# A four-layer scan network on one core: small VectorE operations moved or given PSUM operands, and the C product in three pieces

## The chip, the core and the metric

The kernel runs on one core of a Trainium2 chip. A core has engines that run side by side, each through its own queue in order: TensorE (PE, with weight loads shown apart as PEld), VectorE (DVE), ScalarE (ACT), GpSimd (POOL) and SyncE (SP), which here issues the DMAs. They meet in two memories on the chip: SBUF, and PSUM in eight banks of 512 float32 values per partition, which TensorE writes. The metric is the time of one execution in device microseconds; the time given for a kernel is the median of its runs.

## The reference

The input is 16 images of 192 channels by 32x32 pixels, all in float32. Four residual layers follow each other, each on a group norm of its input (32 groups of 6 channels):

```python
x = x + L0(_gn(x))   # mLSTM block over 1024 tokens, 12 heads of 32; a 3x3 convolution; batch norm; leaky ReLU
x = x + L1(_gn(x))   # Mamba block over 1024 tokens
x = x + L2(_gn(x))   # depthwise 3x3 convolution, batch norm over all images, clip to 0..6
x = x + L3(_gn(x))   # four-direction selective scan, and a local branch, mixed by a router
```

The scans of layers 1 and 3 are one recurrence, for 384 channels d and 16 states n:

```python
dA = jnp.exp(dt_t[..., None] * A)
h = dA * h + (dt_t * x_t)[..., None] * B_t[:, None, :]
y = jnp.einsum('bdn,bn->bd', h, C_t)
```

Layer 1 runs it once per image, layer 3 in four directions (rows and columns, forward and backward). The router of layer 3 is `softmax(x.mean((2, 3)) @ r_w.T + r_b)`, two weights per image, on the normalized image. Batch norm needs every image before any goes on, so layer 0 ends before layer 1 starts, and layer 2 before layer 3.

## The kernel before

**Layer 0** (lines 400 to 885) goes through the tokens in 128 chunks of 128. For each chunk TensorE forms the scores, VectorE multiplies them by the decays (line 765), TensorE sums them with the values into the PSUM tile `num`, and `layer0_norm` (line 833) normalizes each head: mean, square and variance on small 128x12 tiles. `layer0_state` carries a state of 128x396 from chunk to chunk. Fronts, group norms and the convolution are woven in between as side tasks.

**Layers 1 and 3** share `scan_run` (line 954). Its work is a list of steps; one step is one state n of one unit of 512 tokens, so layer 1 has 512 steps (2 units of 16 steps per image) and layer 3 has 2048 (8 units per image, 128 steps). In a step, the 384 channels are three tiles of 128 (t = 0, 1, 2). For each tile:

- ScalarE computes the decay `da` = exp(dt*A), 128x512 (line 991), and x*B in transposed form, `xbt` (line 971);
- TensorE turns `xbt` into the PSUM tile `xb`, three transposes and one product with a diagonal (lines 999, 1002; `xb` has 3 buffers), one step ahead of the scan;
- VectorE runs the recurrence over 512 tokens: `h` from `da` in SBUF and `xb` in PSUM (line 1015);
- GpSimd multiplies the whole `h`, 128x1536, in place by C, whose row for n was spread over the partitions by a DMA into `cb` (line 1022, called by `times_c` after the three scans); before it, it saves the last column as the carry for the next unit if there is one (line 1021);
- TensorE adds `h`, transposed, into the PSUM tile `y` (three banks), 4 transposes of 128x128 at a time (line 1033, `total`), two steps later. `h` has 4 buffers, each free again when `total` has read it.

After 16 steps `u.finish` takes `y` to SBUF (line 1141 on ScalarE in layer 1; line 1483 on ScalarE or 1485, an addition on VectorE, in layer 3). The diagonal for four states is made by GpSimd (line 981).

The order on each engine is what the program writes, but for small moves by the scheduler. The loop of `scan_run` (lines 1048 to 1060) writes scans, decays, turns and totals; between them `side.tick` runs the side tasks at the step numbers with which they were added: the next image's front, convolutions, projections and preparations, and the last image's tail. TensorE's scan work is chained in the written order (`in_order`). All side matmuls go through PSUM tiles named `mm`, of which there are two.

The lines of VectorE that the change touches are: `group_norm` (lines 350 to 379), the group norm's application in layer 0 (554), layer 1's front (1245, 1246, 1251) and tail (1368), layer 3's front (1558, 1562), its router (1697 to 1710) and mixing bias (1579, 1580), and in layer 0 the norm of a chunk (840 to 850) and the state (823 to 829). In layer 3 the front of the next image is a side task at steps 36.5 to 45 of the image before, and router and mixing bias come at step 45.

Of the kernel before, what the change touches and what calls it, by code (L numbers as in the profile page):

```python
# [19 lines left out]
HP = 96  # L20
# [259 lines left out]
class Program:  # L280
# [68 lines left out]
    def group_norm(self, pool, psum, x):  # L349
# [14 lines left out]
        d = pool.tile([HP, 2], F32, name="gnd")  # L364
        nc.vector.tensor_tensor(d, mv[:, :, 0], ps[:HP, :2], SUB)
        q = pool.tile([HP, 2], F32, name="gnq")
        nc.vector.tensor_tensor(q, d, d, MUL)
        nc.vector.tensor_tensor(q, q, mv[:, :, 1], ADD)
        mean = pool.tile([HP, 2], F32, name="gnmean")
        nc.vector.tensor_copy(mean, ps[:HP, :2])  # L370
# [3 lines left out]
        self.main.behind(nc.tensor.matmul(ps[:HP, :2], self.k("group", HP), q, start=True, stop=True))  # L374
# [4 lines left out]
        return mean, r, d  # L379
# [166 lines left out]
    def layer0_image(self, b, sp, bp, psum):  # L546
# [6 lines left out]
        for m in range(2):  # L553
            nc.vector.tensor_scalar(x[:, m], x[:, m], mean[:, m : m + 1], r[:, m : m + 1], SUB, MUL)
# [196 lines left out]
    def layer0_step(self, g, n, chunks, sp, bp, psum):  # L751
# [8 lines left out]
        if k:  # L760
# [27 lines left out]
            num = psum.tile([128, NH, DH + 1], F32, name="num", bufs=1)  # L788
# [20 lines left out]
        if k:  # L809
            self.layer0_norm(k, h, sp, bp)  # L810
            yield

    def layer0_state(self, k, vr, last, bp, psum):
# [3 lines left out]
        for i in range(3):  # L817
# [4 lines left out]
        new = k.state = bp.tile([128, 3, 132], F32, name="state")  # L822
        nc.vector.tensor_tensor(
            new, ps[:, :396].rearrange("p (i d) -> p i d", i=3),
            self.k0("bd")[:, None, :].to_broadcast([128, 3, 132]), MUL,
        )
        if last is not None:
            for i in range(3):
                nc.vector.scalar_tensor_tensor(
                    new[:, i], last.state[:, i], k.unit["dec"][:, i, k.c : k.c + 1], new[:, i], MUL, ADD  # L830
                )

    def layer0_norm(self, k, h, sp, bp):
# [6 lines left out]
        nc.vector.tensor_scalar(mean, mean, 1.0 / DH, None, MUL)  # L840
        hs = k.hs = bp.tile([128, NH, DH], F32, name="hs")
        nc.gpsimd.tensor_tensor(hs, x, mean[:, :, None].to_broadcast([128, NH, DH]), SUB)  # L842
        sq = bp.tile([128, NH, DH], F32, name="sq", bufs=1)
        nc.scalar.activation(sq, hs, AF.Square)
        d = sp.tile([128, NH], F32, name="den")
        nc.vector.tensor_tensor(d, h[:, :, DH], h[:, :, DH], MUL)
        nc.vector.tensor_scalar(d, d, 1.0, EPS, MAX, MUL)  # L847
        var = sp.tile([128, NH], F32, name="mhv")
        nc.vector.tensor_reduce(var, sq, AX.X, ADD)
        nc.vector.scalar_tensor_tensor(var, var, 1.0 / DH, d, MUL, ADD)  # L850
# [102 lines left out]
    def scan_run(self, units, side, bp, psum):  # L953
# [6 lines left out]
        xbt, xb, da, h = {}, {}, {}, {}  # L960
# [46 lines left out]
        def scan(i, t):  # L1007
            u, n = steps[i]
            first = u.carry_in is None
            if t == 0:  # L1010
                h[i] = bp.tile([128, 3, 512], F32, name="h", bufs=4)
# [5 lines left out]
        def times_c(i):  # L1017
# [710 lines left out]
```

## Time and profile before

| | |
|---|---|
| median of 3 runs | 17,061.52 us (17,039.57 to 17,072.65) |
| span of the profiled execution, first to last instruction | 17,013.7 us |
| busy: PE, PEld | 15,545.9 us (91%), 10,952.1 us (64%) |
| busy: VectorE, ScalarE, GpSimd | 13,117.0 (77%), 11,873.8 (70%), 11,405.1 us (67%) |
| mean granted TensorE clock | 0.960 |
| VectorE scans (line 1015) | 7,680, 9,092 us together |
| GpSimd C products (line 1022) | 2,560, 8,866 us, 3,467 ns each |

The profile is of one execution, whose own whole time is not on the page; its span is 47.8 us shorter than the median of the runs, which holds what lies before the first and after the last instruction as well. In a row of the groups, the name of the line and engine is followed by output and inputs, the shapes, the number of instructions, the busy time in all and the mean of one, and then the time that the engine stood idle just before them and what ended it. In a table of stretches, the busy time of each engine stands beside the stretch's length: an engine near 100% of it sets its time. A short operation with a long duration was held up while it was already counted as busy.

### The profile page before, as it was taken

To read this page: it belongs to the slowest core of one execution; us is meant where nothing else is said; L and a number is where in the kernel's file an instruction comes from. 1 tells how busy PE (TensorE), PEld (TensorE's weight loads), DVE (VectorE), ACT (ScalarE), POOL (GpSimd) and SP (SyncE) were. 2 spreads that over 40 slices of the span, in tenths; PEclk is the share of its full clock that TensorE was granted. 3 is DMA by queue.
4 is the path that set the end of the run, shared out by engine and by line. 5 is a ranking of instruction groups with operands and counts; after the bars stand their busy time and mean duration, and the time that the engine had idled before them with its cause. 6 is when DMAs were issued, how large, how long until landed. Compare 5 with 4: busy or idle time off the path is not lost. (4 is left out here: it accounts for less than half of the span.)

```text
span 17013.7 us, 263068 instructions
## 1 busy us (share of the span) xinstructions
PE 15545.9 (91%) x99452; PEld 10952.1 (64%) x99452; DVE 13117.0 (77%) x14795; ACT 11873.8 (70%) x19766; POOL 11405.1 (67%) x5491
## 2 busy tenths in 40 slices
PE   8999999989999999879999999999999999999998
PEld 4444444446666666557777777777777777777777
DVE  4555455447777877668888988888888888888888
ACT  3333333337677777558888888888888888888888
POOL 3434444436555555558888878888887888888888
PEclk8999999989999999989999999999999999999999
DMA  1111111123444444333323323332332333233232
GB/s 52 47 46 46 47 46 43 45 78 108 121 124 124 124 123 124 94 110 99 110 83 100 108 90 96 103 104 88 100 109 85 98 108 95 95 102 108 83 99 66
DMA packets 890140, 1544.64 MB, mean 91 GB/s; under 512 B 83472, under 2 KB 314653, under 8 KB 879530
## 3 DMA queue, kind: packets, MB, share of 16 engines
q1 hardware_dynamic: 888874, 1527.81, 29.5%
q8 instruction: 788, 12.91, 0.3%
q14 instruction: 478, 3.92, 0.1%
HBM read 1284.22 MB, written 243.27 MB: 90 GB/s over the span
## 5 line engine op out<-in xcount | busy, mean ns | idle before, releaser
L1022 POOL TENSOR_TENSOR h<-h,cb 128x1536 f32<-128x1536 f32 x2560 | 8866.4, 3467 | 1531.8 <-DVE h L1015 1020.4
L991 ACT ACTIVATE da<-dt,neg_a 128x512 f32<-128x512 f32 x7680 | 5265.6, 714 | 1549.4 <-DVE h L1015 1499.2
L1015 DVE TENSOR_TENSOR_SCAN h<-da,carry,xb 128x512 f32<-128x512 f32 x3840 | 4648.8, 1262 | 703.1 <-PE xb L1002 619.0
L1033 PE MATMUL y<-const,h 128*128 128x128 f32 x30720 | 4705.2, 276 | 115.6 <-DVE ysum L1485 54.0
L1015 DVE TENSOR_TENSOR_SCAN h<-da,xb 128x512 f32<-128x512 f32 x3840 | 4443.4, 1202 | 431.9 <-PE xb L1002 269.0
L999 PE MATMUL xb<-const,xbt 128*128 128x128 f32 x23040 | 4055.0, 281 | 293.6 <-DVE h L1015 155.7
L971 ACT ACTIVATE xbt<-ut,bt 128x384 f32<-128x384 f32 x7680 | 4168.0, 603 | 220.2 <-PE xb L999 219.5
L1033 PEld LDWEIGHTS y<-const,h 128*128 128x128 f32 x30720 | 3674.0, 143 | 315.3 <-issue 263.1
L999 PEld LDWEIGHTS xb<-const,xbt 128*128 128x128 f32 x23040 | 2749.4, 142 | 1743.1 <-issue 568.6
L1002 PE MATMUL xb<-diag,ut 128*128 128x128 f32 x15360 | 3006.1, 278 | 0.0
L1002 PEld LDWEIGHTS xb<-diag,ut 128*128 128x128 f32 x15360 | 2374.7, 195 | 55.9 <-issue 55.9
L842 POOL TENSOR_TENSOR hs<-h,mhm 128x384 f32<-128x384 f32 x128 | 108.6, 848 | 1567.2 <-DVE den L847 731.8
L981 POOL TENSOR_TENSOR diag<-const,bt 128x512 f32<-128x512 f32 x640 | 681.3, 1065 | 522.6 <-PE xb L1002 331.8
L1021 POOL COPY carry<-h 128x3 f32<-128x3 f32 x1280 | 244.3, 191 | 1167.3 <-DVE h L1015 999.6
L531 PE MATMUL conv<-ya,w_conv 128*64 128x512 f32 (+1 forms) x1152 | 502.2, 647 | 102.8 <-DMA ya<-yrows 57.8
L716 POOL TENSOR_TENSOR e<-e,const 128x1536 f32<-128x1536 f32 x128 | 443.4, 3464 | 223.8 <-DMA e<-row 207.7
L928 PE MATMUL mm<-dbl,w_dt 45*128 45x512 f32 x960 | 537.1, 643 | 49.9 <-DVE dt L932 26.8
L722 ACT ACTIVATE e<-e 128x1536 f32<-128x1536 f32 x128 | 189.8, 1482 | 420.9 <-POOL e L717 420.8
L791 PEld LDWEIGHTS num<-v,p 128*128 128x128 f32 x3072 | 385.7, 200 | 123.0 <-issue 51.2
L1182 PE MATMUL mm<-rep,t_dw 96*32 96x512 f32 x2304 | 432.4, 625 | 23.6 <-DMA rep<-xr 23.5
L1182 PE MATMUL mm<-rep,taps 128*32 128x512 f32 x3072 | 421.9, 609 | 26.1 <-DMA rep<-xr 15.9
L580 PE MATMUL mm<-xn,w_up 96*128 96x512 f32 x768 | 400.6, 667 | 35.9 <-DVE xn L398 28.3
(273 smaller groups left out, 17311.8 us busy)
## 6 DMA issues: line engine op xcount, KB each, us to landing
cb<-row SPq DMA_DIRECT2D x2560, 256.0 KB
rep<-xr SPq DMA_DIRECT2D x384, 331.0 KB
e<-row SPq DMA_DIRECT2D x128, 768.0 KB
rep<-xin SPq DMA_DIRECT2D x384, 256.0 KB
rep<-xr SPq DMA_DIRECT2D x384, 228.8 KB
xr<-xin SPq DMA_DIRECT2D x48, 612.5 KB
xr<-xpad SPq DMA_DIRECT2D x32, 867.0 KB
x<-x SPq DMA_DIRECT2D x32, 768.0 KB
```

Of the source, the lines that this page charges most:

```text
L531: nc.tensor.matmul(o, self.w_c2[:k, t, c0 : c0 + o.shape[0]], src[:k, r0 : r0 + 16, dx : dx + W], start=t == 0, stop=t == 14, skip_group_c ...
L716: nc.gpsimd.tensor_tensor(k.e, k.e, self.k0("mask")[:, None, :].to_broadcast([128, NH, 128]), ADD)
L928: nc.tensor.matmul(ps, w_dt[:, t * 128 : (t + 1) * 128], dbl, start=True, stop=True)
L971: nc.scalar.activation(t[:, c], u.ut[:, c], AF.Copy, scale=u.bt[:, c, n : n + 1])
L981: nc.gpsimd.tensor_tensor(d, ident[:, None, :].to_broadcast([128, 4, 128]), u.bt[:, 3, n : n + 4][:, :, None].to_broadcast([128, 4, 128]), ...
L991: nc.scalar.activation(da[i, t], u.dt[:, t], AF.Exp, scale=u.neg_a(t, n))
L999: in_order(nc.tensor.transpose(xb[i, t][:, c * 128 : (c + 1) * 128], xbt[i][:, c, t * 128 : (t + 1) * 128], ident))
L1002: in_order(nc.tensor.matmul(xb[i, t][:, 384:], u.ut[:, 3, t * 128 : (t + 1) * 128], u.diag[n // 4][:, n % 4], start=True, stop=True, skip_ ...
L1015: nc.vector.tensor_tensor_scan(hv, dv, xv, 0.0 if first else u.carry_in[:, n, t : t + 1], MUL, ADD)
L1022: nc.gpsimd.tensor_tensor(h[i], h[i], u.c.pop(n)[:, None, :].to_broadcast([128, 3, 512]), MUL)
L1033: in_order(nc.tensor.matmul(u.y[:, j], h[i][:, t, c * 128 : (c + 1) * 128], ident, is_transpose=True, start=n == 0 and j % 4 == 0, stop=n ...
L1182: self.nc.tensor.matmul(ps[32 * g : 32 * g + 32], blocks[:, g * side + r], seen, start=r == 0, stop=r == side - 1, skip_group_check=True,)
```

## The change

Five things change. The diff is cut to them.

1. **The C product**: three products of 128x512, each written after its own scan, from `h` into a new tile `hc`. `h` and `hc` have two buffers each, in place of four of `h`. `h` is released by GpSimd's last piece and the carry copy, `hc` by TensorE. The transposes into `y` come one step after the scan in place of two, four for the same t at a time, and `y` is laid out by t first.
2. **Group norm**: difference, square and sum of the small tiles go from VectorE to ScalarE's Square (two of 96x1) and to TensorE, which adds the variance by a second matmul. The mean is kept negated. Applying it goes from VectorE to ScalarE in layer 0 and to GpSimd in layers 1 and 3.
3. **Fronts of layers 1 and 3**: the leaky or clipped branch passes through a PSUM tile `mm`, so that VectorE has one input in SBUF and one in PSUM; layer 1's addition goes to GpSimd.
4. **Router and mixing bias of layer 3**: two-input operations become reductions over two elements, ScalarE steps, and two small GpSimd operations.
5. **Layer 0**: the chunk's mean and one square go to ScalarE; square and sum of squares live in spare columns of the PSUM bank of `num`; the state's decay is applied on the PSUM tile before the mask, not on the SBUF state after it.

```diff
@@ group_norm
-        nc.vector.tensor_tensor(d, mv[:, :, 0], ps[:HP, :2], SUB)
-        nc.vector.tensor_tensor(q, d, d, MUL)
-        nc.vector.tensor_tensor(q, q, mv[:, :, 1], ADD)
+        for m in range(2):
+            nc.scalar.activation(q[:, m : m + 1], ps[:HP, m : m + 1], AF.Square, bias=mv[:, m, 0:1], scale=-1.0)
-        nc.vector.tensor_copy(mean, ps[:HP, :2])
+        nc.vector.tensor_scalar(mean, ps[:HP, :2], -1.0, None, MUL)
...
-        self.main.behind(nc.tensor.matmul(ps[:HP, :2], self.k("group", HP), q, start=True, stop=True))
+        self.main.behind(nc.tensor.matmul(ps[:HP, :2], self.k("group", HP), mv[:, :, 1], start=True, stop=False))
+        self.main.behind(nc.tensor.matmul(ps[:HP, :2], self.k("group", HP), q, start=False, stop=True))
...
@@ layer0_image
-            nc.vector.tensor_scalar(x[:, m], x[:, m], mean[:, m : m + 1], r[:, m : m + 1], SUB, MUL)
+            nc.scalar.activation(shift, mean[:, m : m + 1], AF.Copy, scale=r[:, m : m + 1])
+            nc.scalar.activation(x[:, m], x[:, m], AF.Identity, bias=shift, scale=r[:, m : m + 1])
@@ layer0_state
-        nc.vector.tensor_tensor(
-            new, ps[:, :396].rearrange("p (i d) -> p i d", i=3),
-            self.k0("bd")[:, None, :].to_broadcast([128, 3, 132]), MUL,
-        )
+        add = ps[:, :396].rearrange("p (i d) -> p i d", i=3)
...
-                    new[:, i], last.state[:, i], k.unit["dec"][:, i, k.c : k.c + 1], new[:, i], MUL, ADD
+                    add[:, i], last.state[:, i], k.unit["dec"][:, i, k.c : k.c + 1], add[:, i], MUL, ADD
...
+        nc.vector.tensor_tensor(new, add, self.k0("bd")[:, None, :].to_broadcast([128, 3, 132]), MUL)
@@ layer0_norm
-        nc.vector.tensor_scalar(mean, mean, 1.0 / DH, None, MUL)
+        nc.scalar.activation(mean, mean, AF.Copy, scale=1.0 / DH)
...
+        nc.scalar.activation(n2, h[:, :, DH], AF.Square)
...
-        nc.vector.tensor_tensor(d, h[:, :, DH], h[:, :, DH], MUL)
-        nc.vector.tensor_scalar(d, d, 1.0, EPS, MAX, MUL)
+        nc.vector.tensor_scalar(d, n2, 1.0, EPS, MAX, MUL)
...
-        nc.vector.tensor_reduce(var, sq, AX.X, ADD)
-        nc.vector.scalar_tensor_tensor(var, var, 1.0 / DH, d, MUL, ADD)
+        nc.vector.tensor_reduce(ss, sq, AX.X, ADD)
+        nc.vector.scalar_tensor_tensor(var, ss, 1.0 / DH, d, MUL, ADD)
@@ scan_run
-                h[i] = bp.tile([128, 3, 512], F32, name="h", bufs=4)
+                h[i] = bp.tile([128, 3, 512], F32, name="h", bufs=2)
...
-        def times_c(i):
-            nc.gpsimd.tensor_tensor(h[i], h[i], u.c.pop(n)[:, None, :].to_broadcast([128, 3, 512]), MUL)
+        def times_c(i, t):
+                hc[i] = bp.tile([128, 3, 512], F32, name="hc", bufs=2)
+            nc.gpsimd.tensor_tensor(hc[i][:, t], h[i][:, t], u.c[n], MUL)
...
             for t in range(3):
                 scan(i, t)
+                times_c(i, t)
                 decay(i + 1, t)
                 turn(i + 1, t)
-                total(i - 2, t)
+                total(i - 1, t)
...
-            times_c(i)
@@ layer1_front
+                nc.scalar.activation(ps, v, AF.Copy, scale=0.01)
-                nc.vector.scalar_tensor_tensor(v, v, 0.01, v, MUL, MAX)
-                nc.vector.tensor_tensor(x[:, m, h], x[:, m, h], v, ADD)
+                nc.vector.tensor_tensor(v, v, ps, MAX)
+                nc.gpsimd.tensor_tensor(x[:, m, h], x[:, m, h], v, ADD)
...
-            nc.vector.tensor_scalar(xf[:, m], x[:, m], mean[:, m : m + 1], r[:, m : m + 1], SUB, MUL)
+            nc.gpsimd.tensor_scalar(xf[:, m], x[:, m], mean[:, m : m + 1], r[:, m : m + 1], ADD, MUL)
@@ layer3_front (layer1_tail's last operation alike)
+                nc.scalar.activation(ps, y2[:, h], AF.Relu, bias=self.bn2[:, m, 1:2], scale=self.bn2[:, m, 0:1])
+                nc.vector.scalar_tensor_tensor(x[:, m, h], ps, 6.0, x[:, m, h], MIN, ADD)
...
-            nc.vector.tensor_scalar(
+            nc.gpsimd.tensor_scalar(
                 xpad[:, m, 1 : 1 + W, 1 : 1 + W], x[:, m].rearrange("p (a b) -> p a b", b=W),
...
+        nc.gpsimd.tensor_tensor(xm, d, mean, ADD)
+        nc.gpsimd.tensor_tensor(xm, xm, r, MUL)
@@ layer3_local, router
-        nc.vector.scalar_tensor_tensor(wb, self.v96("3pw_b", 0, 2), wts[:, 1:2], wb, MUL, ADD)
+            nc.scalar.activation(wb[:, m : m + 1], self.v96("3b_out", m), AF.Copy, scale=wts[:, 0:1])
...
-        nc.vector.tensor_tensor(xm, d, r, MUL)
-            nc.vector.tensor_copy(wide, xm[:, m : m + 1].to_broadcast([HP, HP]))
+            nc.scalar.copy(wide, xm[:, m : m + 1].to_broadcast([HP, HP]))
...
-        nc.vector.tensor_tensor(top, e[:, 0:1], e[:, 1:2], MAX)
-        nc.vector.tensor_scalar(e, e, top, None, SUB)
-        nc.scalar.activation(e, e, AF.Exp)
-        nc.vector.tensor_tensor(top, e[:, 0:1], e[:, 1:2], ADD)
+        nc.vector.tensor_reduce(top, e, AX.X, MAX, negate=True)
+        nc.scalar.activation(e, e, AF.Exp, bias=top)
+        nc.vector.tensor_reduce(top, e, AX.X, ADD)
```

## The prediction

> **What bounds the kernel now.** I read the busy time by stage first (layer 0 ends at 3739 us, layer 1's scan run at 7160, layer 3's run goes from 7390 to 16948), then the same table for one image of layer 3, then VectorE and GpSimd in order of time, then the waits. Columns of the table: stretch, its length, busy us of PE, PEld, DVE, ACT, POOL, granted clock, DMA share, GB/s.
>
> ```profile
> 0.00:3739.00 3739.00, 3331.78 (x14599) 1718.78 (x14600) 1841.11 (x3649) 1146.42 (x1733) 1436.26 (x876) 0.91 0.19 49
> 3739.00:7160.00 3421.00, 3152.74 (x19115) 2106.66 (x19115) 2696.69 (x2916) 2458.09 (x4000) 2056.94 (x986) 0.98 0.39 118
> 7390.00:16948.00 9558.00, 8891.84 (x65173) 7064.64 (x65171) 8515.84 (x8122) 8214.00 (x13958) 7883.04 (x3611) 0.98 0.31 97
> ```
>
> Layers 0 and 1 are PE's (89% and 92%). In layer 3, four engines are between 82 and 93% busy, so the bound changes from stretch to stretch. One image of it (128 steps):
>
> ```profile
> 12205.00:12400.00 195.00, 173.01 (x1232) 139.46 (x1231) 170.14 (x167) 173.31 (x290) 159.68 (x77) 0.98 0.24 74
> 12400.00:12447.00 47.00, 34.69 (x232) 31.20 (x230) 46.83 (x49) 31.29 (x57) 32.44 (x19) 0.85 0.38 125
> 12447.00:12744.00 297.00, 294.09 (x2168) 220.54 (x2167) 256.62 (x242) 251.46 (x425) 243.53 (x114) 0.99 0.36 114
> 12744.00:12807.00 63.00, 58.21 (x473) 51.49 (x472) 61.61 (x56) 59.81 (x107) 57.81 (x19) 1.00 0.25 79
> ```
>
> The second row, 8 steps of 5.9 us, is VectorE alone: 46.83 of 47.00. It holds the next image's front, group norm and router. The third is PE's; the last, 16 steps of 3.9 us with little side work, is VectorE's with GpSimd 92% busy. VectorE in the second row, in order of time (start, us, instruction):
>
> ```profile
> 12402.15 3.48 DVE L1558 SCALAR_TENSOR_TENSOR x<-tmp,x 96x512 f32<-96x512 f32 x1
> ...
> 12418.70 1.85 DVE L367 TENSOR_TENSOR gnq<-gnd 96x2 f32<-96x2 f32 x1
> ...
> 12428.90 2.76 DVE L1697 TENSOR_TENSOR xm<-gnd,gnr 96x2 f32<-96x2 f32 x1
> ...
> 12435.46 2.47 DVE L1705 TENSOR_TENSOR rt<-re 96x1 f32<-96x1 f32 x1
> ...
> 12442.09 2.40 DVE L1580 SCALAR_TENSOR_TENSOR wb<-p,re,wb 96x2 f32<-96x2 f32 x1
> ```
>
> Two elements per partition in 2.76 us is a wait, not work: line 1697 alone spreads from 149 to 2775 ns (min/median/max, from its own view), up to the length of GpSimd's long product, which runs meanwhile:
>
> ```profile
> L1697 DVE TENSOR_TENSOR xm<-gnd,gnr x16: 149/2748/2775, 7289.0 to 16036.9; 96x2 f32<-96x2 f32 x16
> ```
>
> The product's price whole, and the nearest row for a piece of it (same engine, operation and 128x512 shape), then four products back to back:
>
> ```profile
> L1022 POOL TENSOR_TENSOR h<-h,cb 128x1536 f32<-128x1536 f32 x2560 | 8866.4, 3467 | 1531.8 <-DVE h L1015 1020.4 <-issue 308.0 <-DMA rep<-xin 39.7
> L1152 POOL TENSOR_TENSOR sz<-sz,o 128x512 f32<-128x512 f32 x96 | 122.3, 1274 | 38.8 <-DVE o L1151 38.5
> ```
>
> ```profile
> 12001.22 13.73 POOL L1022 TENSOR_TENSOR h<-h,cb 128x1536 f32<-128x1536 f32 x4
> ```
>
> **A. Layer 3's front and router.** VectorE loses per image, from its rows over 16 images: line 1558 (64 x 1555 ns, to be 740 like line 1688's PSUM form) 52 us; 1562 42; 1697 39; 1580 and 1579 39; 367 30; 1705 25 (a reduce of 0.17 stays); 1700 10; 1706, 1708 and 1710 10; 365 and 368 4: 252 us, 15.7 per image. The second row's VectorE falls to 31 us. GpSimd gets two 96x1024 operations (between 1.83, scaled from line 717's 2752 ns for 1536, and line 611's 2352; 2.1 taken), two tiny ones (0.19, line 1021) and the pieces' 8 x 0.26 (D): 32.4+4.6+2.1 = 39.1 us. So GpSimd bounds the stretch next, at 39.7 us if it fills 98.5%, as the busiest engine does in the rows beside it: -7.3 us on 15 images (the first front runs before the run, uncontended), -110 us. Ends: 0 (GpSimd comes out late and hands the time on) and -15.7 x 15 = -235.
>
> **B. Layer 1.** Lines 1246, 1251, 1368 and 367 cost VectorE 12.5 us per image there; but PE was 92% busy, and in a stretch with four 1246s in 5.43 us (5208 to 5228) PE was busy 17.5 of 20.0 and VectorE 18.7. I take that 2 us and a little of the tail: -2.3 x 15 = -35; ends 0 and -12.5 x 15 = -188.
>
> **C. Layer 0.** Line 850 (128 x 0.5 us over its median 0.17) and 554 (32 x 1.45 over its unblocked 0.80) give VectorE back 110 us, but it is 49% busy and PE 89%. Against that, mean and square take 256 ScalarE steps at 0.21 us (line 851), which lengthen each chunk's chain by 54 us in all. The state's decay on PSUM keeps an "mm" tile three operations (1.2 us) longer, with 24 matmuls of scores behind it as cover. Taken 0; ends -110 and +54.
>
> **D. The product in pieces.** A piece costs 1.272 (line 1152, in place: I take out of place as equal, no row shows it). Back to back, starts lie 0.05 closer ((13.73-3.47)/3 = 3.42). So 3 x 1.225 = 3.67 in place of 3.42: +0.26 us of GpSimd a step, 650 us in all. What hides it is GpSimd's idle time (18% in layer 3); what breaks the cover is burstiness: a quick step takes VectorE 3.5 us (nine scans in 10.65), while GpSimd needs 3.67 plus 0.26 for the diagonal's share plus, in the units that hand a carry on, 0.27: 3.9 to 4.2. It falls behind 0.4 to 0.7 a step. The h ring, cut from four tiles to two, allows about 2.1 us (three scans less one piece and the carry) before a step's first scan must wait, with VectorE's whole queue behind it. y one step behind is no loss: the first piece is done 1.27 after its scan and asked for a whole step later, where the whole product left some 1.3 us. Laid over the recorded scan ends of all 2,560 steps (a piece starts after its scan and the piece before; a step's first scan waits for the last piece of two steps back; each lack moves everything behind it), starts 1.227 apart lose 84 us, 1.16 apart 4, 1.30 apart 238. I take +84, by the row of the same shape; ends +238 and -73 (PE's 57.2+16.0 us of waits for the whole product, gone).
>
> [...]
>
> **E. New waits.** 128 front tiles (lines 1245, 1558) go through the two-deep "mm" ring between ScalarE and VectorE, and PE queues behind. The like wait, PE for line 932, cost 54 us over 480 tiles: 128 x 0.11 = +14; ends 0 and 128 x 0.74. The stores of x1, xf1 and xpad now wait for GpSimd in SP's queue with the cb loads behind; at its 60% load in layer 1 I cost that at nothing (48 x 2.6, the longest cb wait, if cover fails: 125). One more matmul per group norm: 64 x 2 passes x 0.224 = 29 if bare, +10 taken. The drain is a step and two pieces shorter: -3.
>
> **Sum:** -110-35+0+84+14+10-3 = -40. The profiled span is 17,013.7; the median of the runs, 17,061.5, lies 47.8 above it (start and end), which I leave. 17,061.5-40, rounded: 17,020.
>
> **Rivals.** *GpSimd becomes the bound* (slower): for it, its 92% in the last row above and the halved ring; against it, the 18% idle. Decides when starts of pieces lie over about 1.26 apart: at 1.30, D is +238, A shrinks to -60, B stays: 17,061+238-60-35+24 = 17,230. *The relief is paid in full* (faster): freed VectorE stops delaying scans in layers 0 and 1 too: A -150, B -100, C -50, D +40, the rest +21: -239, so 16,820. For it, the 550 us of VectorE time in A to C; against it, PE at 92%. *Nothing moves*: the engines change places and time hangs on PE (294.09 of 297.00 in the third row): 17,060.
>
> **How the numbers follow.** Forecast case 0.5 (16,900 to 17,070 by itself; of it 0.40 faster, 0.10 within 0.2%, which is about what a measurement tells from no change), GpSimd bound 0.32 (0.02 of it within 0.2%), full relief 0.10, nothing moves 0.08 (0.03 within, 0.05 slower by small costs). Faster 0.50, same 0.15, slower 0.35. The range leaves out the far halves of the outer cases: 16,840 to 17,230.
>
> **What would show it.** A: no VectorE operation of two elements over 0.4 us; the eight front steps at about 40 us, GpSimd the busiest. D: pieces at 1.27 us, GpSimd near 90% in layer 3, and a first scan of a step waiting for GpSimd, 50 to 150 us in all; pieces near 1.1 would make it faster, waits over 250 us slower. E: PE waits for line 1251's successor. C: layer 0 within 60 us of 3,739. Wrong most easily by the piece's price and by how long the front's new GpSimd work holds products up.

## The result and the profile after

| | before | after |
|---|---|---|
| median | 17,050.24 us (12 runs) | 17,031.19 us (12 runs, 17,009.24 to 17,052.04) |
| ratio | | 0.9988 (95% interval 0.9979 to 0.9996) |
| span of the profiled execution | 17,013.7 us | 17,028.0 us |
| layer 0, layer 1, between, layer 3, tail | 3,739, 3,416, 234, 9,554, 70 us | 3,741, 3,430, 236, 9,553, 69 us |

The change takes 19 us off, 0.12%; 40 were forecast. The stages of the two profiled executions hardly differ (layers 1 and 3 are taken from their first scan to the first scan of their last step), so the question is not where the 19 us are but what cancels what. A stage's time is that of one profiled execution: layer 0, whose code is the same in six of the kernels of this document, takes 3,740 to 3,755 us in them, so that 10 us between two stages say little by themselves. A first look is the busy time by stage of the changed kernel, with the same columns as before: stretch, length, busy us of PE, PEld, DVE, ACT, POOL, granted clock, DMA share, GB/s.

```profile
0.00:3741.00 3741.00, 3346.38 (x14638) 1726.58 (x14639) 1612.96 (x3291) 1250.86 (x2092) 1430.60 (x882) 0.91 0.19 49
3741.00:7175.00 3434.00, 3159.53 (x19185) 2088.58 (x19184) 2515.02 (x2720) 2499.98 (x4120) 2327.66 (x2130) 0.98 0.41 118
7406.00:16963.00 9557.00, 8903.37 (x65212) 7053.84 (x65211) 8306.00 (x7937) 8252.77 (x14100) 8411.10 (x7766) 0.98 0.33 97
```

VectorE lost 228 us of work in layer 0, 182 in layer 1 and 210 in layer 3; GpSimd gained 271 and 528 in the last two. The length of every stage stayed. One image of layer 3 in the same four stretches shows that something did move:

```profile
12203.00:12398.00 195.00, 174.22 (x1216) 142.06 (x1215) 169.31 (x166) 172.25 (x288) 170.13 (x157) 0.96 0.25 75
12398.00:12440.00 42.00, 32.61 (x239) 26.43 (x238) 32.26 (x38) 33.43 (x67) 37.89 (x41) 0.97 0.40 129
12440.00:12737.00 297.00, 293.85 (x2171) 221.35 (x2170) 256.61 (x241) 250.95 (x423) 256.35 (x238) 1.00 0.38 116
12737.00:12802.00 65.00, 58.54 (x478) 52.08 (x477) 62.55 (x57) 61.37 (x110) 61.96 (x52) 1.00 0.25 75
```

The front stretch went from 47 to 42 us, and VectorE in it from 46.83 to 32.26. But now no engine fills it: GpSimd, the busiest, has 37.89 of 42.00. The last stretch, quiet steps, is 2 us longer. The small operations of that front in order of time (start, us, instruction) are not held up any more:

```profile
12399.59 0.66 DVE L1563 SCALAR_TENSOR_TENSOR x<-mm,x 96x512 f32<-96x512 f32 x1
...
12427.17 0.15 DVE L1714 TENSOR_REDUCE rt<-re 96x1 f32<-96x2 f32 x1
```

None of VectorE's operations on one or two elements in the group norms and the router takes over 0.16 us in this kernel.

The groups of the changed kernel give the prices of the new operations: a piece of the product 1,279 ns, a branch on VectorE 667, a group norm applied on GpSimd 1,202. In the first line GpSimd's idle time before the pieces is nearly all waiting for TensorE to free `hc`.

```profile
L1022 POOL TENSOR_TENSOR hc<-h,cb 128x512 f32<-128x512 f32 x7680 | 9582.1, 1279 | 1609.6 <-PE y L1038 1460.7 <-DVE h L1016 105.5 <-issue 21.7
...
L1563 DVE SCALAR_TENSOR_TENSOR x<-mm,x 96x512 f32<-96x512 f32 x64 | 42.6, 667 | 37.5 <-ACT mm L1562 37.5
...
L1567 POOL TENSOR_SCALAR xpad<-x,gnmean,gnr 96x1024 f32<-96x1024 f32 x32 | 38.1, 1202 | 0.7 <-ACT gnr L376 0.7
```

The waits (in all, times, longest, us) show what is new. First TensorE's and VectorE's in the changed kernel, then the two of TensorE's that answer them in the kernel before:

```profile
PE mm L1186 <- DMA rep<-xr: 118.9, 41, 11.0
PE y L1038 <- DVE ysum L1491: 102.2, 45, 3.2
...
DVE h L1016 <- POOL hc L1022: 151.7, 146, 4.6
DVE h L1016 <- POOL carry L1027: 95.5, 94, 3.0
```

```profile
PE y L1033 <- DVE ysum L1485: 54.0, 32, 2.7
PE mm L1182 <- DMA rep<-xr: 39.4, 25, 10.0
```

`rep` are the shifted copies of the padded image that the depthwise convolutions of layers 2 and 3 read; they are loaded from `xr`, which is stored from `xpad`. TensorE waits for them three times as long as before, and twice as long for the addition of a finished unit's `y` to the sum (`ysum`).

Cut into 8 steps (first scan to first scan), the mean over images 0 to 14 of layer 3 shows gains at two places and losses at many, in us:

| steps | before | after | difference |
|---|---|---|---|
| 24 to 32 | 38.23 | 33.85 | -4.38 |
| 40 to 48 (front, router) | 46.72 | 42.28 | -4.44 |
| 0 to 8, 64 to 72, 96 to 104 | 120.38 | 123.47 | +3.09 |
| 32 to 40, 48 to 56 | 73.34 | 75.59 | +2.25 |
| 112 to 120 | 31.97 | 33.22 | +1.25 |
| last image, whole | 529.5 | 549.5 | +20.0 |

In layer 1 (images 1 to 14), steps 28 to 32 went from 29.58 to 34.03 us, which is +62 us and more than the stage lost. The experiments take these apart. Their phases are always those of this table.

### The profile page after: what moved, and what is told of

Same layout as the page of the kernel before. It is cut to its first block, busy times and chain, and to the rows that moved or that the text cites. A ratio compares the mean times of both kernels' runs of the same rounds, so it can differ in the third digit from the quotient of the medians.

```text
span 17028.0 us, 269290 instructions
## 1 busy us (share of the span) xinstructions
PE 15578.2 (91%) x99580; PEld 10929.7 (64%) x99580; DVE 12493.1 (73%) x14043; ACT 12059.5 (71%) x20391; POOL 12201.4 (72%) x10803
## 5 line engine op out<-in xcount | busy, mean ns | idle before, releaser
L1022 POOL TENSOR_TENSOR hc<-h,cb 128x512 f32<-128x512 f32 x7680 | 9582.1, 1279 | 1609.6 <-PE y L1038 1460.7
L1038 PE MATMUL y<-const,hc 128*128 128x128 f32 x30720 | 4715.8, 276 | 157.4 <-DVE ysum L1491 102.2
L1038 PEld LDWEIGHTS y<-const,hc 128*128 128x128 f32 x30720 | 3663.2, 143 | 365.8 <-POOL hc L1022 248.6
L393 PE MATMUL mm<-lnsq,const 96*96 96x512 f32 (+1 forms) x576 | 348.2, 689 | 87.0 <-ACT lnsq L392 64.0
```

The source lines that it names most:

```text
L1022: nc.gpsimd.tensor_tensor(hc[i][:, t], h[i][:, t], u.c[n], MUL)
L1038: in_order(nc.tensor.matmul(u.y[:, t, c], hc[i][:, t, c * 128 : (c + 1) * 128], ident, is_transpose=True, start=n == 0 and c == 0, stop=n ...
```

## Experiments: the moves and the pieces, each alone

**The moves alone**: the scan loop of before, everything else as after.

```diff
-            nc.gpsimd.tensor_tensor(hc[i][:, t], h[i][:, t], u.c[n], MUL)
+            nc.gpsimd.tensor_tensor(h[i], h[i], u.c.pop(n)[:, None, :].to_broadcast([128, 3, 512]), MUL)
...
-                total(i - 1, t)
+                total(i - 2, t)
...
+            times_c(i)
```

> The changed kernel with the scan loop of before (one product of 128x1536 in place, y two steps behind, four h buffers); all moves of VectorE's small operations kept. If relief and pieces simply add (my theory), this is 60 to 150 us faster than before: the eight front steps of layer 3 fall from 46.7 to about 40 us per image, and step 24 of an image of layer 3 stays at 11.0 us, since GpSimd's queue is as coarse as before. Rival, the relief is worth little by itself because TensorE takes the place of VectorE: within 30 us of before, front steps at 44 us or more.

**The pieces alone**: the reverse, the kernel before with the scan loop of after.

```diff
-            nc.gpsimd.tensor_tensor(h[i], h[i], u.c.pop(n)[:, None, :].to_broadcast([128, 3, 512]), MUL)
+            nc.gpsimd.tensor_tensor(hc[i][:, t], h[i][:, t], u.c[n], MUL)
...
-                total(i - 2, t)
+                total(i - 1, t)
```

> The kernel before with only the new scan loop (three out-of-place pieces, y one step behind, h and hc two buffers each); VectorE's small operations as before. If relief and pieces add: 40 to 130 us slower than before, step 24 of an image of layer 3 down from 11.0 to about 7.4 us (GpSimd's queue is finer), quiet steps about 1 us longer per 8. Rival, the shorter product already shortens the holds on VectorE: no two-element operation of VectorE over 1.4 us, front steps of layer 3 at 43 us or less, the whole within 30 us of before or faster; then the two halves overlap and their sum is more than the whole.

| | median, us | ratio (95%) | layer 1 | layer 3 | 40 to 48 | 24 to 32 |
|---|---|---|---|---|---|---|
| both (after) | 17,031.19 | 0.9988 (0.9979 to 0.9996) | 3,430 | 9,553 | 42.28 | 33.85 |
| moves alone | 16,942.38 | 0.9939 (0.9926 to 0.9951) | 3,443 | 9,467 | 39.87 | 37.49 |
| pieces alone | 16,976.12 | 0.9961 (0.9948 to 0.9973) | 3,381 | 9,539 | 39.71 | 34.80 |

A ratio is to runs of the kernel before that were taken beside the run; where ratio and medians differ, the ratio counts. Each alone is faster than both together. The front falls to the same 39.8 us by either, but not to the same limit. The front stretch of image 8 with the pieces alone, then with the moves alone:

```profile
12369.00:12409.00 40.00, 31.21 (x219) 27.64 (x219) 39.83 (x50) 27.57 (x50) 33.34 (x34) 0.87 0.43 137
12368.00:12408.00 40.00, 31.20 (x230) 25.03 (x229) 30.98 (x36) 33.20 (x67) 35.92 (x23) 0.97 0.41 131
```

With the pieces alone VectorE still fills the stretch, with less to hold it up. With the moves alone it has 30.98 of 40.00 us, no engine fills the stretch, and TensorE waits in it for the copies `rep`: 4.3 us per image in steps 40 to 48 (mean of images 1 to 14), and nothing with the pieces alone or in the kernel before. Against the kernel before, layer 1 loses 27 us by the moves alone and gains 35 by the pieces alone.

## Experiments: the length of GpSimd's instruction

**Three pieces in place**, after the third scan, on the kernel before: no new tile, four buffers of `h`, `y` two steps behind, no move.

```diff
-            nc.gpsimd.tensor_tensor(h[i], h[i], u.c.pop(n)[:, None, :].to_broadcast([128, 3, 512]), MUL)
+            c_n = u.c.pop(n)
+            for t in range(3):
+                nc.gpsimd.tensor_tensor(h[i][:, t], h[i][:, t], c_n, MUL)
```

> The kernel before with its product split in three in-place pieces after the third scan, everything else as before (four h buffers, y two steps behind). It measures the price of three instructions for one by itself: pieces at 1.27 us. If that price is what the pieces lose: 40 to 100 us slower than before, less what shorter holds give back in layer 3's front (up to 60). If the loss of the new loop comes from its two-deep rings, this one is within 20 us of before or faster.

**Two halves in place**, 128x768 each, the same otherwise.

```diff
+            for s in (slice(0, 256), slice(256, 512)):
+                nc.gpsimd.tensor_tensor(
+                    h[i][:, :, s], h[i][:, :, s], c_n[:, None, s].to_broadcast([128, 3, 256]), MUL
+                )
```

> The kernel before with its product in two in-place halves of 128x768 in place of one of 128x1536, nothing else. Holds of VectorE should be as long as GpSimd's instruction: 1.9 us at most for two elements, against 3.5 with one product and 1.3 with three. If hold length is the cause, it gains between the two: 60 to 130 us faster than before, front steps 40 to 48 of layer 3 at 41 to 44 us. If the finer queue of GpSimd alone is the cause, the front steps stay at 45 us or more.

| | median, us | ratio (95%) | layer 1 | layer 3 | 40 to 48 | 24 to 32 |
|---|---|---|---|---|---|---|
| three in place | 16,903.56 | 0.9912 (0.9897 to 0.9927) | 3,361 | 9,484 | 39.93 | 37.47 |
| two in place | 17,010.95 | 0.9976 (0.9967 to 0.9986) | 3,423 | 9,522 | 43.81 | 38.64 |

Three lines of code in place of one, and the kernel is 0.88% faster with all of VectorE's two-input operations where they were, where the first case above had it 40 to 100 us slower. Two halves gain 0.24%, some 41 us, less than the 60 to 130 forecast; their front steps are as forecast (43.81). The router's first operation, two elements per partition, shows why. The groups of the product and that operation's own view (min/median/max ns), first with two halves, then with three pieces:

```profile
L1024 POOL TENSOR_TENSOR h<-h,cb 128x768 f32<-128x768 f32 x5120 | 9241.8, 1832 | 1297.0 <-issue 822.9 <-DVE h L1015 316.8 <-POOL h L1024 111.1
```

```profile
L1701 DVE TENSOR_TENSOR xm<-gnd,gnr x16: 153/1008/1012, 7296.4 to 16016.5; 96x2 f32<-96x2 f32 x16
```

```profile
L1024 POOL TENSOR_TENSOR h<-h,cb 128x512 f32<-128x512 f32 x7680 | 9615.8, 1284 | 1049.2 <-DVE h L1015 897.9 <-DMA rep<-xin 24.6 <-issue 3.9
```

```profile
L1699 DVE TENSOR_TENSOR xm<-gnd,gnr x16: 148/586/832, 7240.9 to 15917.4; 96x2 f32<-96x2 f32 x16
```

With GpSimd instructions of 3.47, 1.83 and 1.28 us the same operation takes at most 2.78, 1.01 and 0.83 us. It runs into a product that is under way: in all 45 cases with a product running it ends 12 to 20 ns after that product does. In the other three, those of image 0, GpSimd was idle, and it takes 0.15 us. In the kernel before, this is the product beside the VectorE line of 2.76 us at 12428.90 that the prediction shows:

```profile
12428.21 3.44 POOL L1022 TENSOR_TENSOR h<-h,cb 128x1536 f32<-128x1536 f32 x1
```

The longest of all VectorE operations of at most two elements takes 3.39, 1.91 and 1.25 us in the three kernels. The hold, then, is what is left of the instruction that GpSimd is in the middle of. An operation with one input in PSUM did not have it: in the kernel before, image 8, a product runs from 12434.48 to 12437.92 us; the router's operation on one input in PSUM (line 1703, two elements) starts at 12435.29 and takes 0.13 us, and the next, with both inputs in SBUF (line 1705, one element), starts at 12435.46 and takes 2.47, to the end of the product. Over the 16 images line 1703 takes 0.13 us at most, line 1705 2.71. So there are two ways to shorten the hold, to take VectorE's second input from PSUM, or to make GpSimd's instruction short. The second helps at every such operation at once, but leaves some of each hold: in steps 40 to 48 VectorE is busy for 46.3 us before, 39.5 with three pieces in place and 31.3 with the moves alone (means of images 1 to 14).

Steps 24 to 32 gain by another effect of short instructions. In them GpSimd multiplies the last half image's `v` by `sz`, 3.45 us, and TensorE's output projection waits for it. In the kernel before, image 8, this product came behind a whole C product that had been issued before it (GpSimd, then TensorE's projection with its idle time):

```profile
12327.60 3.46 POOL L1022 TENSOR_TENSOR h<-h,cb 128x1536 f32<-128x1536 f32 x1 [3.12 <-issue]
12331.01 3.45 POOL L1677 TENSOR_TENSOR v<-v,tmp 128x1536 f32<-128x1536 f32 x1
```

```profile
12334.51 2.02 PE L1685 MATMUL mm<-v,w_out 128*96 128x512 f32 x2 [4.54 <-POOL v L1677]
```

In the changed kernel it comes behind a single piece, and TensorE waits half as long:

```profile
12325.40 1.27 POOL L1022 TENSOR_TENSOR hc<-h,cb 128x512 f32<-128x512 f32 x1 [1.91 <-DVE h L1016]
12326.63 3.45 POOL L1688 TENSOR_TENSOR v<-v,tmp 128x1536 f32<-128x1536 f32 x1
```

```profile
12330.13 1.10 PE L1696 MATMUL mm<-v,w_out 128*96 128x512 f32 x2 [2.30 <-POOL v L1688]
```

Step 24 alone (mean of images 1 to 14) takes 11.00 us before, 7.41 after, 7.36 with the pieces alone and 11.10 with the moves alone: the gain is the pieces'. It is at step 24 with three pieces in place too (7.82), though part of it comes back at other steps there (37.47 for the eight).

## Experiment: y one step behind

On the three pieces in place, `y` follows the scan by one step, as in the changed kernel.

```diff
-                total(i - 2, t)
+                total(i - 1, t)
```

> The kernel before with three in-place pieces after the third scan and y one step behind the scan in place of two, four h buffers. If y one step behind costs about 1 us per switch of direction because the sum of a finished unit no longer lies beside a burst of side matmuls, the first eight steps of an image of layer 3 are 42 us, as in the changed kernel, and steps 64 to 72 are 44 us; the whole is 50 to 150 us slower than the split alone, more if TensorE also waits for the pieces. Rival, the two-deep rings cost it: then those steps stay at 40.9 and 43.0 us.

17,205.88 us, ratio 1.0095 (1.0081 to 1.0109), 302 us more than with two steps. Most of it belongs to this kernel alone: its pieces start after the third scan, so TensorE finds them unfinished (its waits for line 1024 are 618.9 us, 38.1 with two steps). But one loss is that of the changed kernel. TensorE's waits for the addition of a finished unit, with the pieces and `y` one step behind, and with three pieces in place and `y` two behind:

```profile
PE y L1037 <- DVE ysum L1488: 102.5, 46, 3.2
```

```profile
PE y L1035 <- DVE ysum L1487: 54.4, 32, 3.1
```

With one step behind it is 91.0 in the run here and 102.2 in the changed kernel; 54.0 in the kernel before. Steps 64 to 72 and 96 to 104, which begin with a change of direction, take 1.0 and 1.1 us more in the changed kernel and with the pieces alone, 1.4 and 1.5 more here, and nothing more with two steps behind. For steps 0 to 8, which lose as much in the changed kernel, this run shows no loss (40.51 us): that loss comes with the rest of the new loop, since the pieces alone have it too (42.51). In these two kernels scans wait 0.9 us per image there for GpSimd, in the kernel before and with three pieces in place 0.02.

## Experiments: what layer 1 loses by the moves

**The addition of layer 1's front back on VectorE**, otherwise the changed kernel:

```diff
-                nc.gpsimd.tensor_tensor(x[:, m, h], x[:, m, h], v, ADD)
+                nc.vector.tensor_tensor(x[:, m, h], x[:, m, h], v, ADD)
```

> The changed kernel with one operation moved back: layer 1's front adds the branch on VectorE again, not on GpSimd. My reading of the trace after: VectorE's bn_stats now waits for GpSimd's add, which queues behind pieces and itself waits for VectorE, and so steps 28 to 30 of an image of layer 1 grew by 4 us. Then layer 1 is 30 to 60 us shorter than in the changed kernel. Rival, the loss there comes from the mm tiles that the branch now occupies: layer 1 within 15 us of the changed kernel.

17,053.55 us, ratio 1.0001 (0.9992 to 1.0010); steps 28 to 32 of layer 1 get worse, 35.64 us. GpSimd's addition is not the loss.

**The moves with three pieces in place**: the changed kernel with the loop and the buffers of before, `y` two steps behind, and the product cut as above.

```diff
-            nc.gpsimd.tensor_tensor(hc[i][:, t], h[i][:, t], u.c[n], MUL)
+            c_n = u.c.pop(n)
+            for t in range(3):
+                nc.gpsimd.tensor_tensor(h[i][:, t], h[i][:, t], c_n, MUL)
...
-                total(i - 1, t)
+                total(i - 2, t)
```

> All moves of VectorE's small operations, with the scan loop of before whose product is split in three in-place pieces after the third scan (four h buffers, y two steps behind). Theory now: moving the operations and shortening the product remove the same holds of VectorE, so the two gains (110 and 149 us alone) don't add; the front steps 40 to 48 of layer 3 stay near 39.9 us per image, and layer 1's steps 28 to 32 are 34 us as with the moves alone. Then this is within 40 us of the split alone (16,904), rather above it. Rival, they add and only the new loop spoilt the sum: 16,800 or less.

**The same with layer 1's front as before** (its branch, addition and group norm's application on VectorE; the text below the diff has the application stay on GpSimd, but the diff moves it too):

```diff
-                nc.scalar.activation(ps, v, AF.Copy, scale=0.01)
-                nc.vector.tensor_tensor(v, v, ps, MAX)
-                nc.gpsimd.tensor_tensor(x[:, m, h], x[:, m, h], v, ADD)
+                nc.vector.scalar_tensor_tensor(v, v, 0.01, v, MUL, MAX)
+                nc.vector.tensor_tensor(x[:, m, h], x[:, m, h], v, ADD)
...
-            nc.gpsimd.tensor_scalar(xf[:, m], x[:, m], mean[:, m : m + 1], r[:, m : m + 1], ADD, MUL)
+            nc.vector.tensor_scalar(xf[:, m], x[:, m], mean[:, m : m + 1], r[:, m : m + 1], ADD, MUL)
```

> The same, with layer 1's front as before the change (leaky branch and addition on VectorE from SBUF, no mm tile; only the application of the group norm stays on GpSimd). If that front's new path is what lengthens layer 1's steps 28 to 32 from 29.6 to 34 us, they fall to 30 us or less and the whole is 40 to 75 us faster than the same kernel with the new front. Rival, the group norm's or the tail's moves do it: 33 us or more, no gain.

16,879.68 us (0.9906, 0.9893 to 0.9920) and 16,877.84 (0.9907, 0.9892 to 0.9922). On top of three pieces in place, which give 0.88% alone, all the moves are worth 0.06%, which the intervals do not tell from nothing: layer 3 gains 39 us more (9,445), and layer 1 loses 38 (3,399). Steps 28 to 32 of layer 1 take 32.83 and 31.28 us, 28.40 without the moves; the front accounts for 1.55 of the 4.4.

Layer 3 by itself tells how much of the two gains is the same. With the old loop the moves take 87 us off it, three pieces in place 70, and both together 109: 48 us overlap. With the new loop both together take off 1. The new loop costs layer 3 55 us without the moves (9,539 for 9,484) and 108 with them (9,553 for 9,445). In the front, steps 40 to 48, scans of the changed kernel wait 3.8 us per image for GpSimd's carry copy and pieces; in the kernel before, with the moves alone, with the pieces alone and with three pieces in place they wait there for neither, and in the moves with three in place for 0.2 us. In this last kernel TensorE still waits 2.8 us per image there for the copies, so what the moves could add to short pieces in the front is not seen free of that wait.

What happens in these steps is seen in the trace of the changed kernel. One image of layer 1, four stretches, then VectorE's and TensorE's rows that fall into them:

```profile
5427.00:5433.00 6.00, 2.90 (x24) 2.29 (x22) 4.33 (x5) 5.71 (x11) 6.00 (x6) 1.00 0.94 241
5433.00:5437.00 4.00, 4.00 (x5) 0.48 (x5) 0.00 (x0) 0.00 (x0) 0.83 (x1) 0.51 1.00 254
5437.00:5441.00 4.00, 4.00 (x17) 2.05 (x16) 1.28 (x1) 2.72 (x5) 0.00 (x0) 0.63 0.04 14
5441.00:5445.00 4.00, 4.00 (x31) 2.76 (x31) 1.85 (x2) 2.28 (x5) 0.00 (x0) 1.00 0.17 43
```

```profile
5438.69 1.28 DVE L1016 TENSOR_TENSOR_SCAN h<-da,carry,xb 128x512 f32<-128x512 f32 x1 [7.37 <-PE xb L1003]
```

```profile
5432.98 1.85 PE L1186 MATMUL mm<-rep,t_dw 96*32 96x512 f32 x2 [2.24 <-DMA rep<-xr]
```

TensorE comes to layer 2's depthwise products (line 1186) before the copies have landed and waits 2.24 us, after two shorter gaps of 0.68 and 0.18 us. It is then busy without a break, but with a granted clock of 0.51 for 4 us and 0.63 for 4 more, which comes to half the clock for an estimated 6.9 us. The transposes `xb` of the next step stand behind them in TensorE's queue, and VectorE, with GpSimd and ScalarE after it, waits 7.37 us. Over 14 images the granted clock of steps 28 to 32 is 0.950 before and 0.907 after. The kernel before loses clock there too, in 9 of the 14 images what 1 us or more would be worth, and in 8 of these TensorE waits for the copies for less than 0.6 us; so this wait is not the only thing that lowers the clock.

The longest gap alone does not settle how long the lower clock lasts. Here no gap was longer than 2.24 us, and in the 6 us up to its end TensorE was busy for 2.90; in image 8 of layer 3 of the same kernel a wait of 3.66 us was followed by a granted clock of 0.57 for 4 us (12437 to 12441) and 1.00 after that, which comes to half the clock for an estimated 3.4 us. What sets it is not shown here.

## Experiments: a later first use of the copies

Layer 2 and the local branch of layer 3 are side tasks with fixed step numbers, 26 and 45, and pause after the first loads, for 0.7 and 1.5 steps. Here the first pause is made longer, in the changed kernel, in the moves with three pieces in place, and in the kernel before.

```diff
@@ layer2
-                yield Wait(0.7)
+                yield Wait(0.7 if m or i else 2)
@@ layer3_local
-                yield Wait(1.5)
+                yield Wait(1.5 if m or i else 3)
```

> The changed kernel, with the first use of the replicas put off: in layer 3's local branch the first pause is 3 steps in place of 1.5, in layer 2 it is 2 in place of 0.7. All that is computed stays. Theory 1 (part of the sum is lost because TensorE's queue reaches the depthwise product before the replicas have landed, now that the front before it is shorter): TensorE's waits for the replica loads fall from 118.9 us to 50 or less, steps 28 to 32 of a layer-1 image from 34.0 us to 31 to 32.5, steps 40 to 48 of a layer-3 image from 42.3 to about 41, and the median to 16,960 to 17,000 us. Theory 2 (the wait only stands in for work of other engines that ends just after it): the waits fall likewise, but TensorE then waits for VectorE or GpSimd instead, and the median stays at 17,020 to 17,050.

> The moves together with the product in three pieces in place after the third scan, and the first use of the replicas put off as in the run beside it. Theory 1: TensorE's waits for the replica loads fall from 99.5 us to about 40, layer 1's run from 3,399 us to about 3,370, and the median from 16,880 to 16,800 to 16,850. Theory 2: the median stays at 16,865 to 16,895.

> The kernel before, with the first use of the replicas put off: in layer 2 the first pause is 2 steps in place of 0.7, in layer 3's local branch 3 in place of 1.5. Theory 1 (what the late replicas cost is new with the moves, which end the work ahead of the store later or shorten the stretch between): steps 28 to 32 of a layer-1 image fall from 29.6 us to 28.5 at the most, layer 1's run from 3,416 to about 3,400, and the median from 17,043 to 17,015 to 17,045. Theory 2 (layer 2's fixed step number is too early in the kernel before as well): steps 28 to 32 fall to 26 to 27 us, layer 1's run to 3,350 to 3,370, and the median to 16,970 to 17,000. Layer 3's steps 40 to 48 stay at 46 to 47 us by both.

A fourth kernel tells the engine from the step number: the moves of layer 3 with three pieces in place and the longer pause in layer 3 alone, while layer 1 has its front and the application of its group norms (front and tail) on VectorE as before. Against the kernel with the front as before:

```diff
@@ layer1_tail
-            nc.gpsimd.tensor_scalar(
+            nc.vector.tensor_scalar(
@@ layer3_local
-                yield Wait(1.5)
+                yield Wait(1.5 if m or i else 3)
```

> The same, but layer 1 keeps the application of the group norm on VectorE in front and tail and its front as before, while layer 3 has the moves; only layer 3's first pause is lengthened, to 3 steps. Theory 1 (layer 1 loses because its tail's last operation went to GpSimd and the store behind it starts late): steps 28 to 32 of a layer-1 image come back to 28.5 to 29.5 us from 31.3, layer 1's run to 3,360 to 3,375, and the median to 16,830 to 16,860. Theory 2 (layer 1 loses whatever engine applies the norm, because the fixed step numbers of layer 2 come too early after a shorter tail): steps 28 to 32 stay at 31 to 33 us, layer 1's run at 3,385 to 3,400, and the median is 16,860 to 16,890.

| | median, us | ratio (95%) | layer 1 | layer 3 | layer 1, 28 to 32 | its clock |
|---|---|---|---|---|---|---|
| before | 17,050.24 | 1 | 3,416 | 9,554 | 29.58 | 0.950 |
| before, later | 17,020.97 | 0.9981 (0.9972 to 0.9990) | 3,395 | 9,559 | 27.21 | 0.984 |
| after | 17,031.19 | 0.9988 (0.9979 to 0.9996) | 3,430 | 9,553 | 34.03 | 0.907 |
| after, later | 16,950.31 | 0.9943 (0.9930 to 0.9957) | 3,354 | 9,551 | 27.89 | 0.992 |
| moves, three in place | 16,879.68 | 0.9906 (0.9893 to 0.9920) | 3,399 | 9,445 | 32.83 | 0.919 |
| the same, later | 16,793.50 | 0.9857 (0.9844 to 0.9870) | 3,311 | 9,445 | 26.50 | 1.000 |
| layer 1 back | 16,848.76 | 0.9887 (0.9874 to 0.9901) | 3,375 | 9,440 | 29.49 | 0.925 |

By the ratios the pause takes 0.45% (77 us) off the changed kernel and 0.49% (84 us) off the moves with three pieces, all of it in layer 1; off the kernel before it takes 0.19%. There steps 28 to 32 fall to 27.21 us, between what the two theories gave, while layer 1's run and the median are what the first gave: the place of the depthwise product was a little early before, and the moves made it much more so. The same stretch of the changed kernel with the pause:

```profile
5378.00:5384.00 6.00, 4.96 (x38) 3.83 (x36) 5.89 (x7) 5.75 (x11) 5.10 (x5) 1.00 0.94 252
5384.00:5388.00 4.00, 3.87 (x30) 2.23 (x30) 3.19 (x5) 3.83 (x8) 4.00 (x4) 1.00 1.04 266
5388.00:5392.00 4.00, 3.79 (x32) 2.81 (x26) 2.18 (x5) 4.00 (x8) 1.97 (x2) 1.00 0.72 220
```

The same loads run, and TensorE does its other work meanwhile at a clock of 1.00. TensorE's waits for the copies in layer 1's run fell from 35.8 to 8.8 us, by 27, while the stage lost 76. In steps 28 to 32 alone, which lost 86 us in 14 images, the granted clock is worth an estimated 41 (34.03 us at 0.907 against 27.89 at 0.992). By this estimate the clock cost more than the wait; the remaining 18 us were not taken apart.

With layer 1's operations back on VectorE, the time and the steps come out as the first theory had them: steps 28 to 32 take 29.49 us, 1.8 less than with only the front back, but 1.1 more than the three pieces alone (28.40). The engine is a part, then, 1.8 us in the tail beside the front's 1.55; the later use heals all of it and is the better cure (26.50).

In layer 3 the longer pause did nothing: 9,551 and 9,445 us as before it. It did not move what it was to move. Image 8 of the changed kernel, without and then with the pause:

```profile
12436.91 1.62 PE L1186 MATMUL mm<-rep,t_dw 96*32 96x512 f32 x2 [3.66 <-DMA rep<-xr]
```

```profile
12341.12 1.88 PE L1186 MATMUL mm<-rep,t_dw 96*32 96x512 f32 x2 [3.74 <-DMA rep<-xr]
```

In all 14 images that have this wait, these first two products stand at the same place of TensorE's order in both kernels, behind the same number of `xb` transposes; only those after them come later. Why the pause left them there is not shown. With the pause, the store of `xpad` was issued at 12327.52 and the first load at 12337.92; the load waited 5.0 us for the store to land. So a later use of the copies in layer 3 was not tried, and over the whole run the waits for the copies fell only from 118.9 to 92.4 us in the changed kernel, where 50 or less had been expected.

The best kernel is the moves with the product in three pieces in place, `y` two steps behind, and the later use in layer 2: 16,793.50 us, 1.43% under the kernel before and 1.3% under the changed kernel, by the two ratios.

## Why the prediction was right, and where it was not

Its time was 11 us from the measured one and its sign was right. Of the terms of its sum, A came out by itself and C nearly, B and D had the wrong sign, and E was too small.

- **A, layer 3's front and router (-110).** By itself its number was right: with the moves alone the eight steps fall from 46.72 to 39.87 us, 39.7 forecast, which is -103 over 15 images. The limit that gave the number was not: "GpSimd bounds the stretch next" at 98.5%, but GpSimd is busy for 35.9 of 40.3 us there with the moves alone (37.89 of 42.00 in the changed kernel's image 8), and TensorE waits 4.3 us for the copies, which the sum did not have. So the agreement is partly luck. Its 96x1024 operations were costed at 2.1 us and took 1.20. In company A was -67. The failed step is that A and D were added: VectorE's holds had been read as the price of two-input operations, when they are what is left of GpSimd's instruction, which D shortens, and scans of the changed kernel wait 3.8 us per image for GpSimd in the front, which they do neither with the moves nor with the pieces alone. That an operation of two elements took 2.775 us at most beside a product of 3.467 stood in the prediction; that a shorter product shortens it was not drawn from it.
- **B, layer 1 (-35).** The moves alone lengthened layer 1 by 27 us. The step that failed is that nothing in its sum asked what the moved front and tail make late: the copies for layer 2. With the pause the relief is there: with three pieces in place layer 1 takes 3,361 us without the moves and 3,311 with moves and pause, -50, of which the pause by itself gives 21 in the kernel before. What remains, an estimated 29, is near the 35; three pieces with the pause and without the moves were not run.
- **C, layer 0 (0).** Nearly right: VectorE has 228 us less to do, and the stage went from 3,739 to 3,741 us. Over all kernels of this document layer 0 takes 3,732 us in the mean of the eight that have its moves and 3,747 in the mean of the six that have not, so that some 15 us were gained.
- **D, the pieces (+84).** The price of a piece was right (1,279 ns for 1,272), and so was GpSimd's load (8,411 of 9,557 us, 88%, near 90 forecast). The waits of scans for GpSimd came out above the 50 to 150 us forecast: 247 in all. A loss of the forecast size is there as well: by the ratios the new loop is 0.49%, some 84 us, slower than three pieces in place. Yet the pieces alone come out at -0.39%, since what short pieces free is more: three in place give -0.88%. The step that failed is the model behind the term: it laid the product's starts over the recorded scan ends and let scans only be delayed, so that it could not show what a short instruction frees. The end given for a gain, -73, was made of TensorE's waits for the product and not of VectorE's holds or of the side product that waits behind it.
- **E, new waits (+24).** The ring of `mm` costs little: TensorE's waits for lines 1251 and 1563 add up to 9.7 us. The step that failed is the stores: they were costed at nothing, with 125 us if the cover failed. It failed: the pause takes 77 us off the changed kernel, and 32 off the kernel before. The path was not the one named, the C rows behind the store in SP's queue, but the copies loaded from what was stored, and a clock that was lower after TensorE's wait for them (0.51 and 0.63 for 4 us each in the image shown).
- **Not in the sum at all**: `y` one step behind. It was called no loss, since the first piece is done in time. That held for the pieces, but not for the addition of a finished unit: about +1 us at steps 64 and 96 of each image, some 31 us over 15 images.

So -40 met -19 by luck: the missed gain of the pieces and the missed losses cancel (layer 1, the end of a unit, scans that wait for GpSimd in the front, and the quiet steps with GpSimd behind: +20 in the last image, which has no front). The rivals: GpSimd did not become the bound of layer 3, but the quiet steps do show its price: the last image takes 529.5 us before, 539.3 with three pieces in place and 546.5 with the pieces alone. The first 10 us are the price of pieces, the other 7 come with the new loop, whose rings of two and `y` one step behind were not told apart there; scans wait 18.6 us for GpSimd in this image with the pieces alone, and 0.3 with three in place. The relief was not paid in full, least of all in layer 0.

## What to carry to other kernels

A short VectorE operation that is sometimes nearly as long as GpSimd's instruction (here up to 3.39 us for at most two elements, beside products of 3.47) is worth mending at GpSimd first: cut its long instruction, keep its place and its buffers (0.88% here), and see what of the moves is still worth making (0.06% here). Do not simply add two gains that take away the same wait; ask of each what the other leaves of it. When a stretch gets shorter, work that was put at a fixed step behind a store and a load can come too early: move it back, for here a wait of 2.24 us was followed by half the clock for an estimated 6.9 us, and see in TensorE's order of instructions that it has moved.

## What the runs showed that was not expected

- TensorE's granted clock fell to 0.51 for 4 us and 0.63 for 4 more after a wait of 2.24 us, and mending one such wait per image took 76 us off layer 1, nearly three times the 27 us by which its waits fell.
- Three pieces of 128x512 in place of one product of 128x1536 keep GpSimd busy for 9,616 us, not 8,866, and the kernel is 0.88% faster for it.
- GpSimd applies a group norm to 96x1024 elements in 1.20 us, two scalars per partition, while a product of two tiles with half the elements per partition takes 1.28.
